# Second norm's tiles of the first sequence turned through DRAM instead of on TensorE, its pieces of the first two sequences stored a place later, and the late loads of MLP input and residual issued in turns

## The chip, the cores and the metric

The kernel runs on one core of one Trainium2 chip. A core has TensorE (PE in the profile; its weight loads are PEld), VectorE (DVE), ScalarE (ACT), GpSimd (POOL) and SyncE (SP), which here issues every DMA of the program from one queue, in the order in which the program wrote them. The metric is the device time of one execution in microseconds (us), the median of several runs. Lower is better.

## The reference, cut to what matters

The input x has 4 sequences of 512 tokens with 512 features. Two residual blocks follow each other:

```python
x = x + attn(layernorm(x))          # gated linear attention, 4 heads of 128, chunks of 128 tokens
x = x + mlp(layernorm(x))           # the "second norm" feeds this

# attn, per chunk and head
q, k, v = x@Wq+bq, x@Wk+bk, x@Wv+bv;  k = k / max(norm(k), 1e-12)
alpha = sigmoid(x@Walpha+balpha);  beta = softplus(x@Wbeta+bbeta)
cla   = cumsum(log(alpha + 1e-6)) over the chunk
attn  = (q @ k.T) * beta * exp(cla - cla.T), causal
y     = attn @ v + (q @ state.T) * exp(cla)
state = state * exp(cla_end) + v.T @ (k * beta * exp(cla_end - cla))

# mlp: three matrices held as 4-bit codes with a scale for every 32 inputs
inter = gelu_tanh(x @ Wg.T) * (x @ Wu.T)     # 512 -> 4096
out   = inter @ Wd.T                          # 4096 -> 512
```

Everything is float32.

## The kernel before, in words

**Tiling.** A tile is 128 tokens of 512 features in float32 (256 KB): 4 tiles for each sequence, 16 in all. A chunk of the attention is one tile. `acc` is a tile of the running residual.

**Places.** The order of the work is written out by hand. The attention products of a sequence b are 12: four of v (`product_v`), four of q (`product_q`), four of k (`product_k`). Each is a place p; place 12b+j holds product j of sequence b. After each product, `behind(p)` (L775) issues the rest of the work of that place. The chunk (b, n) runs some places behind its products: `chunk_of(p)` (L748) gives it the three places from 9+12b+3n on. In the first, TensorE transposes k if need be and ScalarE makes the decay factors from a tile of running sums (`chunk_decay`, L599; the sums of the next chunk are loaded there by `load_sums`, those of a sequence's first chunk in product j = 7). In the second, `chunk_scores` (L658) forms q·k and multiplies it by the decay. In the third, `chunk_sums` forms y; `sums` adds it to the residual and stores that as `accd`, and `rest` starts the second norm. Steps can also be put off: `first_of[p]` is done at the beginning of place p (L783), `last_of[p]` at its end (L825).

**The norms.** `norm` (L330) takes statistics of a tile on VectorE and puts a `settle` step on a list; that step normalises the tile into `hn`. Then the tile has to be turned, so that features lie on partitions. There are two ways. Without `way`, the tile goes on the list `turned`, and `turn` (L374) has TensorE transpose its four 128x128 blocks into PSUM (L380) and calls `use`. With `way`, two VectorE instructions (L349) write the normalised tile with its 32-column blocks crossed, `cross` (L307) stores it to a DRAM tile of 512-byte runs (L310), loads it back in four DMAs of 64 KB (L315) two places later, and three places after that `turn_blocks` (L320) has VectorE transpose 32x32 blocks (L326). The first norm of sequences 1 to 3 takes the way through DRAM, and so do some tiles of k. The second norm of all sequences takes TensorE.

**The second norm's `use`** (`second_norm`, L402) splits the turned tile in three pieces whose sum is exact enough for TensorE's rounded float32 format: ScalarE makes `hi` (L406), VectorE `lo` and `mi` (L407, L408). Each piece is at once stored to `h2d` in DRAM (L410). A tile is turned two places after its `rest`, in the second place of the next chunk (`turn("f")` in L766 or L797), and its three stores stand in SyncE's queue at that spot.

**The MLP** (`mlp`, L955) runs in 35 rounds of up to four of the 32 tiles of the hidden layer for one sequence each, sequence i mod 4 in round i. Two of its places lie among the last attention products. `load_x` (L839) loads the 12 pieces of a sequence (3 kinds by 4 feature blocks, `jk`) for the next round, `residual` (L952) the four `acc` tiles. `gate_up` forms a gate and an up product (L853: `pa` from kinds 0 and 1, `pb` from kind 2), `down` the contribution to the output in PSUM (L897), which `add` and `subtract` (L905, L909) bring into `acc`. Round 1 is the first that uses `down`; its four `acc` tiles are loaded in `last` (L966), after the rest of the pieces for round 2.

**SBUF slots.** Tiles of SBUF come from a list of 42 places for one-tile objects (`one_k`, class `Homes`, L94): first freed, first given. A load into a slot waits until the slot's last user is done, which may be a DMA that still stores from it. PSUM has eight banks (L92), used in turns; the eight partial sums of `down` in a round take all of them.

Of the kernel before, what the change touches and what calls it, by code (L numbers as in the profile page):

```python
# [21 lines left out]
P = 128  # L22
# [13 lines left out]
def f32(t):  # L36
    return t.bitcast(F32)
# [3 lines left out]
def tile_gated_linear_attention__then__nvfp4_geglu(  # L41
# [19 lines left out]
    nc = tc.nc  # L61
    B, T, D = x.shape
    H = D // P
    NCH = T // P
# [12 lines left out]
    h2d = [  # L77
        [dram.tile([KC, P, T], F32, tag=f"h2_{b}_{j}", name=f"h2_{b}_{j}") for j in range(3)]
        for b in range(B)
    ]  # L80
# [40 lines left out]
    one_k = Homes("b", 42, [P, T], two_k)  # L121
# [4 lines left out]
    def heads(t):  # L126
        return t.rearrange("p (h d) -> p h d", d=P)
# [153 lines left out]
    def load(src, name):  # L281
        t = one_k.get(name)
        nc.sync.dma_start(f32(t), src)
        return t
# [13 lines left out]
    first_of, last_of = {}, {}  # L298
# [5 lines left out]
    def crossed(t):  # L304
        return t.rearrange("p (w k i) -> p k w i", w=KC, i=32)
# [14 lines left out]
    def turn_blocks(t, *to):  # L320

        new = f32(t).rearrange("p (a k i) -> p k a i", a=KC, i=32)
        done = 0
        for part in to:
            n = part.shape[1]
            nc.vector.transpose(part.rearrange("p k (a j) -> p k a j", j=32), new[:, done : done + n])  # L326
            done += n
        one_k.put(t)

    def norm(src, key, use, parts=1, within=None, way=None):  # L330


        st = small.tile([P, 6], F32, tag="st", name=f"st_{key}")
        nc.vector.bn_stats(st, f32(src))
        if within:
            within()
        mv = small.tile([P, 2], F32, tag="mv", name=f"mv_{key}")
        nc.vector.bn_aggr(mv, st)
        rs = small.tile([P, 1], F32, tag="rs", name=f"rs_{key}")
        nc.vector.tensor_scalar(rs, mv[:, 1:2], 1e-5, None, ALU.add)  # L340
        nc.gpsimd.tensor_tensor(rs, rs, minus_half[:, :1], ALU.pow)

        def settle():

            hn = one_k.get(f"hn_{key}")
            w = D // parts
            if way:
                for c in range(2):
                    nc.vector.tensor_scalar(  # L349
                        crossed(f32(hn)).rearrange("p (c two) w i -> p c two w i", c=2)[:, c],  # L350
                        f32(src).rearrange("p (c w i two) -> p c two w i", c=2, w=KC, two=2)[:, c],
                        mv[:, 0:1], rs, ALU.subtract, ALU.mult,
                    )
                one_k.put(src)
                cross(hn, key, way, place[0] + 1, place[0] + 4)
                one_k.put(hn)
                return
            for cols in (slice(i * w, (i + 1) * w) for i in range(parts)):
                nc.vector.tensor_scalar(
                    f32(hn)[:, cols].rearrange("p (c two j) -> p c two j", two=2, j=P),  # L360
                    f32(src)[:, cols].rearrange("p (c j two) -> p c two j", two=2, j=P),
                    mv[:, 0:1], rs, ALU.subtract, ALU.mult,
                )
            one_k.put(src)
            turned.append((hn, key, use))

        settled.append(settle)
# [34 lines left out]
    def second_norm(b, n, src):  # L402
        def use(tp):
            g = [one_k.get(f"g{j}_{b}_{n}") for j in range(3)]
            hi, lo, mi = g
            nc.scalar.activation(hi, tp, AF.Copy, scale=HI)  # L406
            nc.vector.tensor_tensor(lo, tp, f32(hi), ALU.subtract)  # L407
            nc.vector.scalar_tensor_tensor(mi, f32(hi), ONE_E, tp, ALU.mult, ALU.subtract)  # L408
            for j in range(3):
                nc.sync.dma_start(  # L410
                    h2d[b][j][:, :, n * P : (n + 1) * P].rearrange("k p t -> p k t"), heads(f32(g[j]))
                )
            one_k.put(*g)

        norm(src, f"f{b}_{n}", use)


    zs, ss = {}, {}
# [321 lines left out]
    for b in range(1, B):  # L740
        for n in range(NCH):
            p = 3 * NCH * (b - 1) + 3 * n - 1 if b > 1 else 2 + 3 * max(n - 1, 0)
# [3 lines left out]
    place, met, summed = [0], set(), []  # L746
# [92 lines left out]
    def load_x(i, which):  # L839
        if i < len(rounds):  # L840
            for j, k in which:
                x3[i].append(load(h2d[i % B][j][k], f"x_{i}_{j}_{k}"))
# [109 lines left out]
    def residual(i, which=range(NCH)):  # L952
        return [load(accd[i % B * NCH + n], f"acc_{i}_{n}") for n in which]

    def mlp():  # L955
        for i, r in enumerate(rounds):
            ts = range(i % B * NCH, (i % B + 1) * NCH)
            ms = tiles[i]
            inter = []
            a4 = residual(i) if i > 1 else None  # L960
            ahead = [0] if i >= B - 1 else [i] if i > 0 else []
            for q, mt in enumerate(ms):
                if q in ahead:
                    load_x(i + 1, jk[: 8 if i == 1 else 6])

                def last():  # L966

                    if q == len(ms) - 1:
                        one_k.put(*x3[i])
                        rest = jk[len(x3[i + 1]) :] if i + 1 < len(rounds) else []  # L970
                        if i == 1:

                            nonlocal a4
                            load_x(i + 1, rest)
                            a4 = residual(i)
                        else:
                            load_x(i + 1, rest)


                some = ((2, 0), (3, 2))[q] if i == 1 else (1, 1)  # L980
                inter.append((yield from gate_up(mt, x3[i], some, r + MC, last, f"{i}_{mt}", mt == ms[-1] and len(ms) < 3)))
                if mt == r and mt < tiles[-1][0]:
                    two_k.put(*wgu[mt])
            final = i + B >= len(rounds)
            dst = [of[t * P : (t + 1) * P, :] if final else accd[t] for t in ts]
            if i == 0:
                over = ms, inter
                continue
            if i == B:
                ms, inter = over[0] + ms, over[1] + inter  # L990
            down(ms, inter, a4, dst, f"{i}", i == len(rounds) - 1)
            if r >= 0 and r % 2 == 1 and r < tiles[-1][0]:
                two_k.put(*wd[r // 2])
            yield


    with tc.manual_schedule():
# [45 lines left out]
        p = 0  # L1043
# [95 lines left out]
```

## Time and profile before

| | |
|---|---|
| median of 3 runs | 1303.22 us (1302.1 to 1303.25) |
| the profiled execution | 1301.6 us, its span 1299.9 us |
| PE busy | 1288.6 us, 99% of the span |
| PEld / DVE busy | 1030.6 us (79%) / 968.1 us (74%) |
| ACT / POOL busy | 452.2 us (35%) / 113.5 us (9%) |
| mean granted TensorE clock | 0.998 |
| DMA | 250.24 MB, mean 193 GB/s |

The span runs from the first to the last instruction of the profiled execution; 1.7 us of its time lie around it. The page of the profile lists the chain of work that ended last, followed back from the last instruction. In the views quoted below, a group of instructions is named by its line of the kernel, its engine and operation, and the tiles that it writes and reads (`tp_f<-ident,hn_f` are the transposes of the second norm, `g` its pieces, `h` their store in DRAM, `x<-h` the MLP's loads of them, `sums<-rows` the loads of running sums, `acc<-acc` the loads of the residual). Times count from the span's start. "Busy" of PE is of modelled, overlapping matmuls.

The last tile of the second norm is turned at 280.4 us, beside the first rounds of the MLP; from there to the end the rounds repeat.

### The profile page before, as it was taken

To read this page: it belongs to the slowest core of one execution; us is meant where nothing else is said; L and a number is where in the kernel's file an instruction comes from. 1 tells how busy PE (TensorE), PEld (TensorE's weight loads), DVE (VectorE), ACT (ScalarE), POOL (GpSimd) and SP (SyncE) were. 2 spreads that over 40 slices of the span, in tenths; PEclk is the share of its full clock that TensorE was granted. 3 is DMA by queue.
4 is the path that set the end of the run, shared out by engine and by line. 5 is a ranking of instruction groups with operands and counts; after the bars stand their busy time and mean duration, and the time that the engine had idled before them with its cause. 6 is when DMAs were issued, how large, how long until landed. Compare 5 with 4: busy or idle time off the path is not lost.

```text
span 1299.9 us, 17044 instructions
## 1 busy us (share of the span) xinstructions
PE 1288.6 (99%) x5736; PEld 1030.6 (79%) x5736; DVE 968.1 (74%) x1581; ACT 452.2 (35%) x878; POOL 113.5 (9%) x179
## 2 busy tenths in 40 slices
PE   9999999999999999999999999999999999999998
PEld 6667576778888888888888888888888888887886
DVE  4577865877777777777777777777777777777566
ACT  2333335743333333333333333333333333332332
POOL 1526462400000000000000000000000000000000
PEclk9999999999999999999999999999999999999999
DMA  6556667976565656555555565656555555555473
GB/s 208 163 163 191 196 191 226 310 263 213 179 195 178 194 178 194 178 195 178 194 178 194 178 194 179 195 178 194 179 194 179 192 181 190 182 179 199 167 253 126
DMA packets 195383, 250.24 MB, mean 193 GB/s; under 512 B 16672, under 2 KB 93792, under 8 KB 195296
## 3 DMA queue, kind: packets, MB, share of 16 engines
q1 hardware_dynamic: 195296, 249.16, 59.3%
q8 instruction: 45, 0.74, 0.2%
q14 instruction: 42, 0.34, 0.1%
HBM read 191.91 MB, written 57.18 MB: 192 GB/s over the span
## 4 chain that ended last, share of the span: by engine, by line
PE 95%; DVE 2%; DMA 1%; ACT 1%; issue 0%; SPq 0%; POOL 0%; DVEq 0%; ACTq 0%; POOLq 0%
PE pa L853 35%; PE p_d L897 26%; PE pb L853 18%; PE pq L450 4%; PE pk L474 3%; PE pva L425 2%; PE pvb L432 2%; PE yp L717 1%; PE sp L663 1%; PE yp L719 1%; PE dp L688 1%; PE tp_f L380 0%; DMA sums<-rows 0%; DMA acc<-acc 0%; DMA x<-h 0%
## 5 line engine op out<-in xcount | busy, mean ns | idle before, releaser
L853 PE MATMUL pa<-x,wgu 128*128 128x512 f32 x2048 | 508.5, 390 | 0.1
L853 PEld LDWEIGHTS pa<-x,wgu 128*128 128x128 f32 x2048 | 384.7, 188 | 80.0 <-DVE acc L909 0.4
L897 PE MATMUL p_d<-wd,i 128*128 128x512 f32 x1542 | 357.3, 389 | 2.3 <-DVE xr L726 0.6
L897 PEld LDWEIGHTS p_d<-wd,i 128*128 128x128 f32 x1542 | 288.2, 188 | 65.8 <-DVE i L877 2.1
L858 ACT ACTIVATE t<-pb 128x512 f32<-128x512 f32 x256 | 151.2, 591 | 357.9 <-PE pb L853 354.0
L853 PE MATMUL pb<-x,wgu 128*128 128x512 f32 x1024 | 273.7, 389 | 0.0
L859 DVE TENSOR_TENSOR t<-pa,t 128x512 f32<-128x512 f32 x256 | 176.4, 689 | 81.7 <-ACT t L858 76.4
L853 PEld LDWEIGHTS pb<-x,wgu 128*128 128x128 f32 x1024 | 192.3, 188 | 40.2
L905 DVE SCALAR_TENSOR_TENSOR acc<-p_d,acc 128x512 f32<-128x512 f32 (+1 forms) x137 | 93.3, 681 | 127.4 <-PE p_d L897 124.0
L873 ACT ACTIVATE i<-t 128x512 fp32r<-128x512 f32 x128 | 81.1, 634 | 194.2 <-DVE t L870 191.1
L865 ACT ACTIVATE t<-t 128x512 f32<-128x512 f32 x128 | 81.1, 634 | 136.0 <-DVE t L859 136.0
L877 DVE TENSOR_TENSOR i<-t,i 128x512 fp32r<-128x512 f32 x128 | 88.3, 690 | 26.0 <-ACT i L873 24.2
L909 DVE TENSOR_TENSOR acc<-acc,p_d 128x512 f32<-128x512 f32 x135 | 92.8, 688 | 14.4 <-PE p_d L897 0.5
L870 DVE SCALAR_TENSOR_TENSOR t<-t,t 128x512 f32<-128x512 f32 x128 | 88.6, 692 | 4.3
L928 POOL TENSOR_TENSOR acc<-acc,last 128x512 f32<-128x512 f32 x1 | 1.3, 1295 | 1015.1 <-ACT last L927 1015.1
L878 DVE SCALAR_TENSOR_TENSOR i<-i,t 128x512 fp32r<-128x512 f32 x128 | 88.9, 694 | 0.0
L450 PE MATMUL pq<-hT,wq 128*128 128x512 f32 x128 | 57.6, 595 | 0.0
L474 PE MATMUL pk<-wk,hT 128*128 128x512 f32 x128 | 57.4, 592 | 0.0
L450 PEld LDWEIGHTS pq<-hT,wq 128*128 128x128 f32 x128 | 23.6, 190 | 24.1 <-issue 23.9
L474 PEld LDWEIGHTS pk<-wk,hT 128*128 128x128 f32 x128 | 23.2, 190 | 23.9 <-issue 23.9
L183 DVE TENSOR_TENSOR wgu<-wgu,wgu 128x1024 fp32r<-128x1024 f32 x32 | 38.9, 1215 | 0.0
L180 DVE SCALAR_TENSOR_TENSOR wgu<-wgu,w_gu 128x1024 fp32r<-128x1024 f32 x32 | 38.9, 1215 | 0.0
(120 smaller groups left out, 901.6 us busy)
## 6 DMA issues: line engine op xcount, KB each, us to landing
x<-h SPq DMA_DIRECT2D x420, 256.0 KB
acc<-acc SPq DMA_DIRECT2D x256, 256.0 KB
h<-g SPq DMA_DIRECT2D x48, 256.0 KB
x<-in_x SPq DMA_DIRECT2D x16, 256.0 KB
pk_gu<-in_gate_p SPq DMA_DIRECT2D x32, 128.0 KB
sc_gu<-in_gate_s SPq DMA_DIRECT2D x64, 64.0 KB
pk_gu<-in_up_p SPq DMA_DIRECT2D x32, 128.0 KB
sc_gu<-in_up_s SPq DMA_DIRECT2D x64, 64.0 KB
```

The costliest lines, as they stand in the source:

```text
L450: nc.tensor.matmul(pq, f32(wq[k // 2])[:, k % 2, h * P : (h + 1) * P], f32(hT[b][k // 2])[:, k % 2, :], start=(k == 0), stop=(k == KC - 1),)
L474: nc.tensor.matmul(pk, f32(hT[b][k // 2])[:, k % 2, n * P : (n + 1) * P], f32(wk[k // 2])[:, k % 2, :], start=(k == 0), stop=(k == KC - 1),)
L853: nc.tensor.matmul(o, w3[j][:, k % 2, c * P : (c + 1) * P], x[j * KC + k], start=(j == js[0] and k == 0), stop=(j == js[-1] and k == KC - 1),)
L858: nc.scalar.activation(f32(t), pb, AF.Copy, scale=-1.0 / ONE_E)
L859: nc.vector.tensor_tensor(f32(t), pa, f32(t), ALU.add)
L865: nc.scalar.activation(f32(g), f32(g), AF.Gelu_apprx_tanh, scale=ONE_E)
L870: nc.vector.scalar_tensor_tensor(f32(u), f32(g), ONE_E, f32(u), ALU.mult, ALU.mult)
L877: nc.vector.tensor_tensor(il, f32(u), f32(ih), ALU.subtract)
L878: nc.vector.scalar_tensor_tensor(im, f32(ih), ONE_E, f32(u), ALU.mult, ALU.subtract)
L897: nc.tensor.matmul(banks[key_][:, part], inter[i][j][:, n * P : (n + 1) * P], wd[ms[i] // 2][j][:, ms[i] % 2, part], start=(i == 0 and j i ...
L905: nc.vector.scalar_tensor_tensor(a, banks[n, False, part.start][:, part], ONE_E, a, ALU.mult, ALU.add)
L909: nc.vector.tensor_tensor(a, a, banks[n, True, 0], ALU.subtract)
```

## The change

1. The second norm of sequence 0 gets a `way`: its four tiles are normalised by the two crossed instructions, stored to DRAM, loaded back in four DMAs each, and turned by VectorE into a new tile `h2T`, from which `use` makes the pieces. The second norm of the other three sequences is still turned on TensorE.
2. The three stores of the pieces are a step of their own. For sequences 0 and 1 it is put at the beginning of the next place, and the pieces' slots are freed there; for sequences 2 and 3 it is done at once, as before.
3. In round 1 of the MLP, the last four pieces of `x` for round 2 and the four `acc` tiles are loaded two and two in turns. Before, all four pieces were loaded ahead of the four `acc` tiles.

```diff
-            for j in range(3):
-                nc.sync.dma_start(
-                    h2d[b][j][:, :, n * P : (n + 1) * P].rearrange("k p t -> p k t"), heads(f32(g[j]))
-                )
-            one_k.put(*g)
-
-        norm(src, f"f{b}_{n}", use)
+
+            def store():
+                for j in range(3):
+                    nc.sync.dma_start(
+                        h2d[b][j][:, :, n * P : (n + 1) * P].rearrange("k p t -> p k t"), heads(f32(g[j]))
+                    )
+                one_k.put(*g)
+
+
+            if b < 2:
+                first_of.setdefault(place[0], []).append(store)
+            else:
+                store()
+
+        def way(t):
+            whole = one_k.get(f"h2T_{b}_{n}")
+            turn_blocks(t, heads(f32(whole)))
+            use(f32(whole))
+            one_k.put(whole)
+
+        norm(src, f"f{b}_{n}", use, way=way if b < 1 else None)
...
-                            load_x(i + 1, rest)
-                            a4 = residual(i)
+                            a4 = []
+                            for s in range(0, NCH, 2):
+                                load_x(i + 1, rest[s : s + 2])
+                                a4 += residual(i, range(s, s + 2))
```

## The prediction

> **What bounds the kernel.** The page first, its slices and its chain:
>
> ```profile
> PE   9999999999999999999999999999999999999998
> ...
> PE 95%; DVE 2%; DMA 1%; ACT 1%; issue 0%; SPq 0%; POOL 0%; DVEq 0%; ACTq 0%; POOLq 0%
> ```
>
> TensorE sets the time. So an edit is worth TensorE work taken from a stretch that the chain spends on PE, or a stall of PE that goes; all else costs nothing until it makes PE wait. Next the chain in order of time, where a piece's second number is its us:
>
> ```profile
> 60.09 1.73 PE pvb L432 x8
> 61.81 0.44 PE tp_f L380 x4
> 62.25 0.89 PE sp L663 x8
> ```
>
> Pieces join without a gap: four transposes are charged 0.44. Sequence 0's other three tiles stand so at 76.27, 91.55 and 105.41. From 7 us to 155 us no other engine is on the chain. Two later places leave PE. The first, at 155 to 169 us, in the chain and in SP's timeline:
>
> ```profile
> 155.89 2.75 SPq L410 DMA_DIRECT2D h<-g  x3
> 158.73 0.69 SPq L579 DMA_DIRECT2D sums<-rows  x1
> ```
>
> ```profile
> 158.73 5.16 DMA sums<-rows
> ...
> 168.14 0.69 DVE dm L674
> 168.83 0.04 issue
> 168.87 1.16 PE yp L717 x8
> ```
>
> The first sums of sequence 2 are issued only behind three stores of pieces, which took SP 2.75 us. They land at 163.89; decay, pieces and scores follow late, and y's eight matmuls take 1.16 where the same piece takes 0.89 at 111.07. With the short gap before them PE loses some 0.4 us. The second, at 255 to 268 us, in the timeline (in brackets the idle time before, and who ended it) and in the busy times by stretch (PE, PEld, DVE, ACT and POOL busy; the last three numbers are granted clock, DMA share and GB/s):
>
> ```profile
> 255.72 2.26 SPq L283 DMA_DIRECT2D x<-h  x4
> 258.03 1.85 SPq L283 DMA_DIRECT2D acc<-acc  x4
> 262.87 0.69 DVE L905 SCALAR_TENSOR_TENSOR acc<-p_d,acc 128x512 f32<-128x512 f32 x1 [3.43 <-DMA acc<-acc]
> 263.62 0.66 PE L593 MATMUL tpk<-ident,k 128*128 128x128 f32 x4 [2.57 <-DVE acc L905]
> 264.41 3.68 PE L853 MATMUL pa<-x,wgu 128*128 128x512 f32 x8
> 270.09 2.10 PE L853 MATMUL pa<-x,wgu 128*128 128x512 f32 x8
> ```
>
> ```profile
> 260.00:262.00 2.00, 1.04 (x5) 0.54 (x3) 0.00 (x0) 0.00 (x0) 0.07 (x1) 1.00 0.97 316
> 262.00:264.00 2.00, 0.39 (x4) 0.39 (x4) 1.03 (x2) 0.00 (x0) 0.00 (x0) 1.00 0.94 324
> 264.00:266.00 2.00, 1.86 (x7) 1.34 (x6) 1.90 (x4) 1.68 (x2) 0.00 (x0) 0.62 0.69 260
> 266.00:268.00 2.00, 2.00 (x7) 1.54 (x6) 1.79 (x4) 1.99 (x6) 0.45 (x1) 0.53 0.36 136
> ```
>
> Round 1's partial sums hold all eight PSUM banks; the next transposes wait 2.57 us for the first `add`, which waits for the first `acc` tile, issued behind four pieces of x while the DMA engines are full (share 0.94 to 0.97). Then the clock drops to half for 3.4 us (0.62 and 0.53 over two stretches of 2 us: 0.76 + 0.94 us lost), so eight matmuls take 3.68 instead of about 1.85.
>
> **Part 1, the turning.** Removed from PE: 16 transposes, four pieces of 0.44: **1.76 us**, all on the path. Two durations compete for a transpose: the group row of L380 has 273 ns mean, and the Trainium skill ("TensorE: Matmul & The Clock Gate", Part 4) gives some 275 ns in a kernel's context, which would make 16 x 0.275 = 4.4 us. But that is latency; transposes overlap, and the chain charges 0.44 / 4 = 0.11 us each. I take 1.76.
>
> Added for each tile: VectorE two L349 (470 ns) for one L359 (574), plus one transpose of 128x512 (L326 on kT: 701), pieces from SBUF instead of PSUM at no difference (L877/L878: 690 and 694, against 689 and 676): 0.37 + 0.70 + 0.02 = 1.09 us, 4.4 us for four. VectorE is busy 54.97 of the 72.90 us from 57.5 to 130.4, so it has 17.9 us to hide this in; uncovered it costs 4.4. ScalarE +0.04 a tile (L873 634 against L406 593). SP one store (L310, 0.38) and four loads (L315, 2.25 together): 2.6 us a tile, 10.5 in all, where its issues fill 50.9 of the same 72.9 us. DMA 0.5 MB a tile, 2 MB in 60 us on top of 163 to 196 GB/s: 33 GB/s more, below the 310 that a slice reaches. The order on VectorE helps: the pieces of sequence 0 no longer stand ahead of `dm` (L407 and L408, 1.37 us before L674) but behind it, at the place's end.
>
> The skill speaks against this part: "VectorE: DVE Perf Modes", "The three transpose paths", warns that a strided DMA copy for a transpose is 19 times slower than the DMA's own transposer. Here the copy only moves 512-byte runs and VectorE turns inside blocks; the trace's own store waits 61.47 to 65.64 for its four loads to begin, 4.2 us, with three more places until the turning. By the rule, at 19 times the section's 1.3 us, an estimate of 25 us for one block, the transposes at the head of VectorE's queue would come some 10 us late (three places are about 14 us) and hold PE up by as much, 40 us for four tiles; by the row they are in time and the sum is as above. I take the row.
>
> **Part 2, the stores.** At 155.89 the three stores leave the spot ahead of the sums, which so issue up to 2.8 us earlier and the stall at 168.8 goes: **0.4 us**. In their new spot the stores stand ahead of `accd`'s store and the way stores, which wait for later VectorE work anyhow; sums of the following chunk come behind them, with three places of slack. Pieces hold three slots a place longer. Readers of `h2d` come much later (x<-h from 199.5 us). Bounds: 0 to 0.5.
>
> **Part 3, the turns.** Moved: two x pieces go behind two `acc` tiles. The first `acc` takes over the spot of the third piece (issued at 257.19 in the trace) and its slot: 0.84 us earlier in issue than 258.03. In transfers two of 256 KB fewer lie ahead; at 316 to 324 GB/s each is 0.82 us, so 1.64 us. Lower bound 0.84 (issue alone), upper 1.64 + 0.2. I take **1.65**, since the full DMA engines set the landing. What is late next: the last two x pieces, now landing where `acc` 0 and 1 did, about 262.8 and 263.6; their first reader, `pb`, would start near 264.5, so some 0.9 us cover it, and a miss costs the miss.
>
> Does the clock's 1.7 us come back too? The skill ("TensorE: Matmul & The Clock Gate", Part 1) has the gate close after an idle window of some 3.4 us; here it closed after 2.57 us of wait, so the measurement decides that less is enough, while 0.9 us may leave it open. By the page's wording this wait was never the cause and the 1.7 stays. It hardly matters: if the clock stays up, PE meets the next `hn_f` (L359), which VectorE reaches only after its eight adds (268.44, done 269.17; the transposes begin 269.63). Adds 1.2 to 1.65 us earlier plus 0.46 of slack give 1.7 to 2.1. So both ways come out near 1.65, up to 2.1.
>
> **Sum.** 1.76 + 0.4 + 1.65 = 3.8 us. The profiled execution took 1301.6 (span 1299.9, 1.7 around it) and would take 1297.8. It stands 1.6 below the median, for which I subtract the same: 1303.2 - 3.8 = **1299.4 us**, its own range 1298.0 to 1300.6.
>
> **The rivals.** *Part 3 is hidden.* VectorE was late before (PE waits 0.44 and 0.59 us for it at 255.8 and 257.1), `acc` transfers share the engines with later ones, or the late x pieces hold up `pb`. Then 1.76 + 0.4 stay: 1301.1. For it: `acc` 0 and later loads run beside each other on 16 engines; against it: the 3.43 us wait names `acc` alone. Chance 0.2.
>
> *More than counted.* The earlier `dm`, the open clock and a calmer SP add up, with the upper bounds: 1.76 + 0.5 + 2.1, and one more half-clock window of 1.7, which could be what the median has over the profiled execution: 6.1, so 1297.1. Chance 0.1.
>
> *The change doesn't do what it says:* PE waits elsewhere for what it no longer transposes (banks, sums), and no stall is moved: 1303. Chance 0.1.
>
> *Slower: SP's queue.* In place 19 eight way loads instead of four stand ahead of sequence 1's first sums. They had landed by 102.69, when ACT's L608 began; POOL reached the mask L612 only at 106.04 (held by kw and vb, so 2.1 us of cover), and `dm`, moved ahead of the pieces, could end 3.4 us before y's matmuls at 110.8. From 5.4 us of delay on PE idles microsecond for microsecond, with a half-clock window (1.7) behind it. I count 2.25 us for four more loads minus 2.8 for the three stores that leave, so no delay; but the loads wait for landings, 4.2 us at most today, with two tiles at once perhaps 1 more. With the 3.8 gained, slower by 0.2% needs 3.8 + 2.6 - 1.7 = 4.7 us of idling, a delay of 10.1; 1306 to 1308. Chance 0.1.
>
> **How the numbers follow.** Some 0.2% (2.6 us) is what a measurement here can tell from no change. The likeliest case has 0.5, with 0.1 for more: faster 0.6. Hidden and nothing: same 0.3. Slower 0.1. The range leaves out half of the slower case and the tail of the fastest: 1297.0 to 1303.4.
>
> **What would show it.** Right: L380's tp_f x48 and no chain piece of it before 117 us; L326 on a new tile x4 at about 0.7; no `sums<-rows` in the chain at 158; the wait of L905 for `acc` under 2 us, and either a clock of 1.00 at 264 or a wait for hn_f. Wrong: PE waiting for `dm` or `sums` between 90 and 130 us, a `pb` that waits for x<-h near 264, or a half-clock window at a new place.

## The result, and the profile after

The changed kernel takes **1315.27 us** in the median (1313.94 to 1315.82), beside 1302.66 (1301.81 to 1303.25) for the kernel before in the same session: a ratio of **1.0098, 95% interval 1.0086 to 1.011**. It is slower by 12.6 us where the prediction had it faster by 3.8, and it lies 12 us above the predicted range. The profiled execution took 1313.94 us, with a span of 1312.2 (1301.6 and 1299.9 before).

Lines of the kernel behind the edit move down by 14: L425 is now L439, L674 is L688, L717 is L731, L905 is L919. L310, L315, L326, L359 and L380 stay; the store of pieces, L410, is L412.

The page of the kernel after, its slices, the clock's slices and the chain's shares by engine:

```profile
PE   9998899989999999999999999999999999999998
...
PEclk9999899999999999999999999999999999999999
...
PE 90%; DMA 5%; DVE 2%; SPq 1%; ACT 1%; issue 1%; POOL 0%; DVEq 0%; ACTq 0%; POOLq 0%
...
L439 PE MATMUL pva<-wva,hT 128*128 128x264 f32 x128 | 33.2, 405 | 10.4 <-DVE hT L326 10.0
```

Before, every slice but the last was a 9, and PE had 95% of the chain. Now the fourth and fifth slices are an 8 (98 to 164 us), and so is the ninth (262 to 295, part 3's place); the clock dips in the fifth (131 to 164), and DMA's share of the chain has gone from 1 to 5%. One group names the cause: PE waits 10.0 us for `hT`, once.

To sum it up, I took for each matmul the time from the end of the matmul before it to its own end, less the median of that for its form; what is left over is PE's lost time. It is 11.58 us before and 25.41 after, 13.83 more. Less the transposes that are gone (L380 has 64 of them instead of 80; 16 x 0.109 = 1.75), and with 0.27 more of tail, that is the 12.3 us between the spans. Of the added loss 11.9 us lie at one place, 135 to 140 us, and 0.8 near 115; the region of part 3 (250 to 285 us) loses 8.5 where it lost 7.4.

That place, in the chain in order of time (start, us, what):

```profile
126.03 0.57 SPq L412
...
126.64 4.64 DMA h<-g
...
131.47 0.72 DVE h2T L326
...
134.31 1.52 DVE g L408
135.84 0.36 DVE hT L326
...
136.24 3.89 PE pva L439 x8
```

and in the timeline (in brackets the idle time before, and who ended it):

```profile
122.90 0.69 DVE L688 TENSOR_TENSOR dm<-sp,dm 128x512 f32<-128x512 f32 x1
125.84 0.39 PE L733 MATMUL yp<-state,qc 128*128 128x128 f32 x2
131.47 0.71 DVE L326 STREAM_TRANSPOSE h2T<-way_f 128x512 f32<-128x512 f32 x1 [7.88 <-DMA h<-g]
135.76 0.76 DVE L326 STREAM_TRANSPOSE hT<-way_a 128x256 f32<-128x256 f32 x2
136.24 3.89 PE L439 MATMUL pva<-wva,hT 128*128 128x264 f32 x8 [10.01 <-DVE hT L326]
```

Read it from below. PE's next product needs `hT` of sequence 2, which VectorE turns at the end of a place. In VectorE's timeline the new turning of tile 3 of sequence 0 into `h2T` stands ahead of it. That waits 7.88 us, and not for its data: for a *store of pieces*. Following the list of free tiles through the program gives the reason: `h2T` of tile 3 is handed the slot of the `lo` piece of tile 2, which the program gave back when the store was queued. The store is issued only at 126.64 and lands at 131.28. Then the eight matmuls take 3.89 us instead of the 1.78 of before (126.77 to 128.55, with no wait ahead of them), as the clock is at half (us of the stretch; busy PE, PEld, DVE, ACT, POOL; granted clock, DMA share, GB/s):

```profile
134.00:136.00 2.00, 0.00 (x0) 0.00 (x0) 2.00 (x3) 1.80 (x5) 1.29 (x1) 0.50 0.11 33
136.00:138.00 2.00, 1.76 (x4) 1.45 (x5) 2.00 (x8) 0.00 (x0) 0.00 (x0) 0.50 0.39 104
138.00:140.00 2.00, 2.00 (x6) 1.49 (x6) 1.90 (x5) 0.00 (x0) 0.30 (x1) 0.50 0.68 233
```

Why was the store so late? SP's timeline after, and then before, at the same part of the program (the last column counts the issues of the row):

```profile
109.59 0.98 SPq L310 DMA_DIRECT2D way_f<-hn_f  x1
...
114.99 2.27 SPq L315 DMA_DIRECT2D way_f<-way_f  x4
117.37 2.70 SPq L315 DMA_DIRECT2D way_a<-way_a  x4
...
121.73 4.20 SPq L315 DMA_DIRECT2D way_k<-way_k  x4
126.03 2.30 SPq L412 DMA_DIRECT2D h<-g  x3
...
129.66 0.56 SPq L593 DMA_DIRECT2D sums<-rows  x1
```

```profile
110.78 2.28 SPq L315 DMA_DIRECT2D way_a<-way_a  x4
113.16 2.81 SPq L410 DMA_DIRECT2D h<-g  x3
...
121.95 0.51 SPq L579 DMA_DIRECT2D sums<-rows  x1
```

The same load of sums is issued 7.7 us later than before, at 129.66 instead of 121.95. The delay adds up from tile to tile: at the five loads of sums from 62 us on it is 0.8, 1.8, 3.3, 6.9 and 7.7 us. I use the last of these loads below as a mark of how late SP is. The waits of SP's queue from 57.5 to 130.4 us, the longest of before and of after (us in total, times, longest):

```profile
SPq L315 <- DMA way_a<-hn_a: 16.3, 5, 4.2
```

```profile
SPq L315 <- DMA way_f<-hn_f: 9.3, 4, 2.7
```

Before, SP stood 16.3 us at the head of its queue until the first norm's tiles had landed; these are part of the time that the prediction took for free. After, the loads of the new tiles wait there instead, 9.3 us, and those of the first norm, which come behind them, find their tiles landed.

From the loads of k at 57.4 us to the mark, SP's timeline adds up to 45.3 us of issues and 19.2 of standing before, 58.2 and 14.1 after. So the issues grew by 12.8 us (11.4 of them the 20 new DMAs), and the standing gave back only 5.1: that is the delay of 7.7.

### The profile page after: what moved, and what is told of

Its sections match the earlier page's. It is cut to its first block, busy times and chain, and to the rows that moved or that the text cites. A ratio compares the mean times of both kernels' runs of the same rounds, so it can differ in the third digit from the quotient of the medians.

```text
span 1312.2 us, 17054 instructions
## 1 busy us (share of the span) xinstructions
PE 1290.0 (98%) x5720; PEld 1031.2 (79%) x5720; DVE 974.9 (74%) x1589; ACT 452.4 (34%) x878; POOL 112.3 (9%) x179
## 4 chain that ended last, share of the span: by engine, by line
PE 90%; DMA 5%; DVE 2%; SPq 1%; ACT 1%; issue 1%; POOL 0%; DVEq 0%; ACTq 0%; POOLq 0%
PE pa L867 35%; PE p_d L911 25%; PE pb L867 17%; PE pq L464 3%; PE pk L488 3%; PE pva L439 2%; DMA x<-h 2%; PE pvb L446 2%; DMA h<-g 2%; SPq L315 1%; PE sp L677 1%; PE yp L731 1%; DMA x<-in_x 1%; PE yp L733 0%; PE dp L702 0%
## 5 line engine op out<-in xcount | busy, mean ns | idle before, releaser
L919 DVE SCALAR_TENSOR_TENSOR acc<-p_d,acc 128x512 f32<-128x512 f32 (+1 forms) x137 | 93.4, 683 | 127.7 <-PE p_d L911 123.5
L488 PE MATMUL pk<-wk,hT 128*128 128x512 f32 x128 | 57.4, 593 | 0.0
L439 PE MATMUL pva<-wva,hT 128*128 128x264 f32 x128 | 33.2, 405 | 10.4 <-DVE hT L326 10.0
```

The lines of the kernel that those rows point to most:

```text
L488: nc.tensor.matmul(pk, f32(hT[b][k // 2])[:, k % 2, n * P : (n + 1) * P], f32(wk[k // 2])[:, k % 2, :], start=(k == 0), stop=(k == KC - 1),)
L919: nc.vector.scalar_tensor_tensor(a, banks[n, False, part.start][:, part], ONE_E, a, ALU.mult, ALU.add)
```

## The experiments

Times are medians; the ratios are against the kernel before in the same session (1301.8 to 1303.1 us), and can differ a little from the quotient of the two medians.

### The three parts, one at a time

**Part 3 alone** (the kernel before with this edit only):

```diff
-                            load_x(i + 1, rest)
-                            a4 = residual(i)
+                            a4 = []
+                            for s in range(0, NCH, 2):
+                                load_x(i + 1, rest[s : s + 2])
+                                a4 += residual(i, range(s, s + 2))
```

> Part 3 alone on the kernel before (late x pieces and residual loaded two and two). The prediction's step says 1.65 us faster: ratio 0.9987, the wait of the first add for acc down from 3.4 to under 2 us. The rival from the changed kernel's trace: the first acc tile takes over the slot of the third x piece with that slot's wait for a store of pieces to land, so its load starts at most 0.8 us earlier and lands no earlier behind as many transfers: between 0.5 us faster and 1.5 us slower, the wait still 3 us or more.

Measured: 1300.94 us, ratio 0.9985 (0.9974 to 0.9996): 1.6 us faster by the medians, 2.0 by the ratio; span 1299.1. Its timeline and stretches, at the spot where the kernel before waited for `acc` and then ran at half clock:

```profile
261.94 0.69 DVE L905 SCALAR_TENSOR_TENSOR acc<-p_d,acc 128x512 f32<-128x512 f32 x1 [0.97 <-PE p_d L897]
262.69 0.66 PE L593 MATMUL tpk<-ident,k 128*128 128x128 f32 x4
268.98 0.66 PE L380 MATMUL tp_f<-ident,hn_f 128*128 128x128 f32 x4 [1.60 <-DVE hn_f L359]
```

```profile
264.00:266.00 2.00, 2.00 (x10) 1.63 (x10) 1.33 (x3) 1.99 (x4) 0.00 (x0) 1.00 1.03 394
266.00:268.00 2.00, 1.38 (x11) 1.11 (x9) 1.79 (x4) 1.56 (x4) 1.37 (x3) 1.00 0.64 246
```

The first `add` waits for PE and no longer for `acc`, the transposes behind it wait for nothing, the clock stays at 1.00, and PE meets `hn_f` 1.60 us early: what the prediction described.

**Part 2 alone** (the stores of sequences 0 and 1 as a step of the next place, the second norm on TensorE):

```diff
-        norm(src, f"f{b}_{n}", use, way=way if b < 1 else None)
+        norm(src, f"f{b}_{n}", use, way=None)
```

with part 3 undone as well.

> Part 2 alone: the second norm is turned on TensorE throughout, only the stores of the pieces of sequences 0 and 1 stand a place later. The prediction's step says 0.4 us faster (0.9997): no wait for the first sums of sequence 2. If the later stores themselves keep slots busy (stores in flight when the slot is written again), PE waits somewhere between 60 and 180 us and it is slower by 1 us or more.

Measured: 1301.72 us, ratio 0.9994 (0.9987 to 1.0001), span 1299.6; the 0.47 us lost at 165 us are gone from the profile. The size agrees with the 0.4 predicted; a ratio of 1 is not excluded.

**Part 1 alone** (stores at once, part 3 undone):

```diff
-            if b < 2:
+            if b < 0:
                 first_of.setdefault(place[0], []).append(store)
```

> Part 1 alone: sequence 0's second norm through DRAM, its stores at once. The prediction's step says 1.76 us faster. Slot theory (the stall of 10 us needs a late store and a slot taken back two places later): the stores are issued a place earlier, some 5 us, so the stall at sequence 2's first v product shrinks to 5 us or less and the time is 3 to 6 us above before. Queue theory (SyncE is full: the way loads wait for the way stores): stores that wait for their pieces in the queue make it later still, the stall stays at 8 us or more, 9 to 14 us above before.

Measured: 1316.6 us, ratio 1.0103 (1.0081 to 1.0125). The whole loss is here. The stall has other places: PE loses 8.4 us near 130 and 5.0 near 165. Its waits, and the longest wait of VectorE:

```profile
PE yp L731 <- DVE dm L688: 9.8, 3, 6.0
```

```profile
128.10 0.69 DVE L407 TENSOR_TENSOR g<-tp_f,g 128x512 fp32r<-128x512 f32 x1 [6.39 <-DMA h<-g]
```

Again a new tile, here a piece, whose slot a store still reads.

**Parts 1 and 2**, without part 3.

> Parts 1 and 2 without part 3. Both theories of the stall: it is all there, about 10 us of wait of PE for hT at the first v product of sequence 2 and 1.7 us of half clock; the time is that of the changed kernel less what part 3 costs, 1313 to 1316 us, 10 to 13 us above before.

Measured: 1317.85 us, ratio 1.0109 (1.0089 to 1.0129): the stall of the changed kernel, 10.0 us of PE for `hT` and 7.9 of `h2T` for a store. Against it the whole change (1.0098) is 1.4 us faster by the ratios, which is less than their noise (about 3 us): whether parts 2 and 3 gain inside the change isn't shown by the times.

**Parts 2 and 3**, the changed kernel with part 1 undone by the edit shown for part 2:

> Parts 2 and 3 of the change without part 1: no tile of the second norm goes through DRAM. The gains measured alone were 0.8 (part 2, stores a place later) and 1.6 us (part 3, turns), at places 90 us apart, so they should add: 2.4 us below the kernel before, near 1300.2, ratio 0.998. If part 3's gain needs the queue as it was in the kernel before, only one of them shows: 1301 to 1302 us. If part 2 is what hurts in the changed kernel: over 1305 us.

Measured: 1299.74 us, ratio **0.9977 (0.9964 to 0.999)**: 3.0 us faster than before, and the fastest version here with the right output. Its runs lie apart: six at 1299.0 to 1299.8 us, five at 1300.4 to 1303.8, the profiled one (1302.21) among the latter.

So part 1 costs some 13 us by itself (0.0103 x 1302.5 = 13.4). Two explanations stood at this point: A, tiles are handed out while a store still reads them; B, SP's queue is late, whatever tile is handed out.

### Which of the two: tiles, or SP's queue

**Tiles handed out later.** The changed kernel, but a tile that a DMA read last comes back to the list four places later:

```diff
+        def put_late(self, p, *ts):
+            for t in ts:
+                _, tag, whole = self.used.pop(id(t))
+                self.late.append((p, tag))
+
+        def age(self, p):
+            while self.late and (p - self.late[0][0] >= 4):
+                self.free.append(self.late.pop(0)[1])
...
-                one_k.put(*g)
+                one_k.put_late(place[0], *g) if b < 2 else one_k.put(*g)
```

(also for the sources and rows of tiles that go through DRAM; `get` takes a late tile when no other is free, and `age` is called at every place)

> The changed kernel in full, but a tile that a DMA was the last to read (pieces of sequences 0 and 1, sources and rows of the way tiles) comes back to the pool only four places later, or when nothing else is free. Same instructions on every queue, so SP stays as full and as late as in the changed kernel (its stores for tile 2 some 12 us behind PE). Theory A (what stalls is the reuse of a tile whose store is still on its way): the transpose into h2T of tile 3 no longer waits 7.9 us for a store, PE's wait for hT goes from 10.0 to under 2 us, the half-clock window behind it goes too: 1302 to 1305 us. Theory B (SP's queue is late, whatever tile is handed out): something else that SP brings late takes the stall's place, PE still loses 8 us or more between 110 and 140, 1311 to 1316 us.

Measured: 1316.28 us, ratio 1.0091 (1.007 to 1.0111). The wait for `hT` falls to 1.1 us, as A had it, but nothing is won. PE's and SP's waits in this kernel:

```profile
PE yp L743 <- DVE dm L700: 11.4, 3, 9.3
```

```profile
SPq L327 <- DMA way_f<-hn_f: 9.8, 4, 3.1
```

PE now waits 9.3 us for a `dm` that ends at 166 us. Behind it, the chain of this kernel goes through loads that SP issues:

```profile
151.17 5.33 DMA sc_gu<-in_gate_s
156.51 2.07 SPq L327
...
159.79 4.89 DMA xr<-in_x
...
165.53 0.61 DVE dm L700
```

The load of `xr` is issued at 159.79, where the kernel with part 2 alone issues it at 147.24, and the mark stands at 132.46. Tile reuse decides where the stall falls, not that there is one. A as the only cause is out.

**Loads a place later.** The changed kernel with

```diff
-                cross(hn, key, way, place[0] + 1, place[0] + 4)
+                cross(hn, key, way, place[0] + (2 if key[0] == "f" else 1), place[0] + 4)
```

> The changed kernel in full, but the four loads that bring a tile of the second norm back are issued one place (about 4.6 us) later, when its store has landed. Theory B in its form 'loads at the head of SP's queue wait for the way store to land': the 2.7 us waits of these loads go, SP catches up by about 2.7 us a tile, the stores of tile 2 are issued some 5 to 8 us earlier, and PE's wait for hT falls from 10.0 to under 4 us: 1303 to 1309 us. If SP is late only by the number of its issues (so many more DMAs a tile): SP stays as late, 1312 to 1316 us.

Measured: 1320.51 us, ratio 1.0126 (1.0102 to 1.0149): worse. SP's and VectorE's waits:

```profile
SPq L315 <- DMA way_a<-hn_a: 11.8, 4, 3.4
```

```profile
DVE h2T L326 <- DMA way_f<-way_f: 9.0, 2, 4.9
```

The edit didn't take a wait away: the next loads in the queue, the first norm's, wait for their own landing at the same spot (11.8 us where the changed kernel has 3.2 for them from 58 to 140 us). And the loads are now so late that VectorE waits for them. My expectation overlooked who stands next in the queue.

**Another queue.** The changed kernel with the new store and loads issued by ScalarE, the loads at the end of their place:

```diff
-        nc.sync.dma_start(way.rearrange("w p m -> p w m"), f32(src).rearrange("p (w m) -> p w m", m=P))
+        other = key[0] == "f"
+        queue_of = nc.scalar if other else nc.sync
+        queue_of.dma_start(way.rearrange("w p m -> p w m"), f32(src).rearrange("p (w m) -> p w m", m=P))
```

(the loads likewise)

> The changed kernel in full, but the way store and the four loads of the second norm's tiles are issued from ScalarE's queue, the loads at the end of their place. The DMA traffic is the same, SP's queue is as in the kernel before. Theory B (SP's queue): SP no longer falls behind, the stores of tile 2 are issued near 113 us as before, the stall for hT goes, 1300 to 1304 us, unless ScalarE, held by the loads' waits, is late for PE itself. Theory C (the 2 MB more of traffic slow every landing): PE still waits 8 us or more, 1311 to 1316 us.

Measured: 1318.69 us, ratio 1.0112 (1.0088 to 1.0135). PE's waits:

```profile
PE sp L679 <- ACT kT L612: 5.1, 2, 4.2
PE rps L576 <- ACT la L558: 4.7, 1, 4.7
```

The wait goes where the DMAs go: now it is ScalarE that comes late to its copy of k and to its logarithm. SP isn't on time either: it issues the fourth of the loads of sums at 116.33, where it was 104.75 before. So the run fits a queue held by loads, but it doesn't separate it from the traffic. The next runs do.

### Part 1 taken apart

**The DMAs alone.** The kernel before, with the transposes on TensorE, plus the store and four loads of each tile into a tile that nobody reads:

```diff
             turned.append((hn, key, use))
+            if key[:2] == "f0":
+                cross(hn, key, one_k.put, place[0] + 1, place[0] + 4)
```

> The kernel before, with the transposes of sequence 0 left on TensorE and their pieces as they were, plus only the DMAs of part 1: for each of the four tiles the store of its rows and, a place later, the four loads into a tile of the pool, which is given back three places later unread. VectorE and TensorE do nothing new; the output is unchanged. Theory B (SP's queue, filled by these 20 DMAs and the waits ahead of them): PE loses 10 us or more between 90 and 170, 1312 to 1320 us. Theory E (VectorE's 4.4 us of added work, and the later order of its pieces, are what is late): no more than 1 us, 1302.5 to 1304 us.

Measured: 1320.04 us, ratio 1.0136 (1.0116 to 1.0155). Twenty DMAs on whose data nothing waits cost 17.7 us (0.0136 x 1302.5). PE's waits and SP's:

```profile
PE yp L719 <- DVE dm L676: 9.6, 3, 5.4
```

```profile
SPq L315 <- DMA way_f<-hn_f: 9.7, 4, 2.8
```

**No DMAs.** Part 1 alone, with the tile kept in SBUF and turned there; it leaves out the exchange of blocks, so the values are in the wrong order:

```diff
-                cross(hn, key, way, place[0] + 1, place[0] + 4)
-                one_k.put(hn)
+                if key[0] == "f":
+                    last_of.setdefault(place[0] + 4, []).append(lambda: way(hn))
+                else:
+                    cross(hn, key, way, place[0] + 1, place[0] + 4)
+                    one_k.put(hn)
```

> Part 1 alone, without its DMAs: the normalised tile stays in SBUF and VectorE turns it inside its 32x32 blocks at the same place, but its blocks are not exchanged, so the second norm's values of sequence 0 are in the wrong order. TensorE does not transpose, VectorE and ScalarE do all that part 1 gives them; SP's queue is as in the kernel before. Theory B: only the 1.76 us that the prediction counted on TensorE remain, with the SP stall at 165 us as before: 1301 to 1302.5 us. Theory E: VectorE's added work alone makes PE wait 8 us or more, 1310 to 1316 us.

Measured: 1306.33 us, ratio 1.003 (1.0015 to 1.0045): 3.9 us slower, between the two expectations. Most of the loss goes with the DMAs, but the 1.76 us don't show either. VectorE's waits show tile reuse again (the tile held in SBUF takes a slot longer):

```profile
DVE g L410 <- DMA h<-g: 5.6, 2, 3.2
```

**Loads that don't wait.** Part 1 alone with all its DMAs, but the loads read the input (so the second norm's values are wrong):

```diff
+                block = way[:, a * 32 : (a + 1) * 32, :]
+                if key[0] == "f":
+                    block = tile_of(0)[:, a * P : (a + 1) * P].rearrange("(w r) m -> w r m", w=KC)
-                nc.sync.dma_start(f32(t)[:, a * P : (a + 1) * P], way[:, a * 32 : (a + 1) * 32, :])
+                nc.sync.dma_start(f32(t)[:, a * P : (a + 1) * P], block)
```

> Part 1 alone, with all of its DMAs in their places, but the four loads of a tile read 64 KB each of the input x instead of the tile just stored, so they need not wait for its landing; the second norm's values of sequence 0 are wrong. As many issues on SP and as much traffic as in part 1 alone. Theory B1 (the wait for the store's landing at the head of SP's queue, 9.0 us in four places, is what makes SP late): it goes, 1301 to 1306 us. Theory B2 (the number of issues, some 10 us of SP's time, is enough): 1310 to 1317 us.

Measured: 1307.95 us, ratio 1.0048 (1.003 to 1.0066). With the same number of DMAs and the same bytes, 8.7 us of part 1's loss are gone by the medians, 7.2 by the ratios, and SP is on time: the timeline of SP here has the mark at

```profile
121.23 0.56 SPq L596 DMA_DIRECT2D sums<-rows  x1
```

where it stands at 121.95 before, at 130.80 in part 1 alone, and at 132.16 with the DMAs alone. This is the strongest reading: with as many DMAs, SP is late only where their loads wait for a store's landing at the head of its queue. Loads that don't wait are issued while the first norm's tiles land, for which SP stands only 4.5 us between the loads of k and the mark, where it stood 13.3 before. From those loads to the mark SP needs 9.2 us less than in part 1 alone: 3.7 less of standing and 5.5 less of issuing, for the same 88 issues. Why these take less time when no load waits isn't shown. 1307.95 lies just above the 1301 to 1306 expected for B1, so something else remains.

### Are the two together the whole cause?

The changed kernel with the later tiles (as above), **and no DMAs** for part 1:

> The changed kernel in full, but without part 1's DMAs (blocks of sequence 0's second norm turned, but not exchanged, so its values are in the wrong order), and with tiles that a DMA read last handed out four places later. VectorE does all of part 1's work. Two-cause theory: the 3.8 us that remained without the DMAs were tile reuse, so nothing waits for a store of pieces any more; parts 2 and 3 give 2.8 us as measured together, part 1 its 1.76: 1298 to 1299.5 us. Theory E (VectorE's added 4.4 us are late by themselves): 1302 to 1306 us.

Measured: 1303.14 us, ratio 1.0002 (0.9989 to 1.0016). The profiled execution took 1298.85, with only 1.4 us lost near 150 us, as the two-cause theory expected, but it is the shortest of twelve; the others reach from 1299.2 to 1305.9. **The same kernel, profiled again:**

> The changed kernel without part 1's DMAs and with tiles handed out later, profiled again. If its executions differ by what happens between 57 and 175 us (part 1's places), the profile of an execution above 1302 us shows PE losing 2 us or more there, waiting for dm or hT; if by part 3's place, the loss is between 250 and 285 us.

Measured: 1299.32 us, again one of the short executions; it loses 1 us near 150. What the longer ones lose is in no trace, but the mean clock of each run is on record: 0.995 to 0.999 in the eight above 1302 us, 1.0 in three of the four below and 0.998 in the other. The means differ by 0.0022, an estimate of 2.9 us out of the 4.6 between the two groups. So the longer ones ran in part at half clock; behind which waits stays open, and with it whether the two causes are the whole.

The later tiles **and loads that don't wait**:

> The changed kernel in full, but the four loads of a tile read the input x (they wait for no landing; the second norm's values of sequence 0 are wrong), and tiles that a DMA read last are handed out four places later. All of part 1's issues and traffic and all its VectorE work stay. Two-cause theory: both causes are gone, PE loses no more than 1 us between 90 and 170: 1298 to 1301 us. If the number of issues (10 us of SP) or the traffic counts by itself: 1304 us or more.

Measured: 1306.21 us, ratio 1.002 (1.0004 to 1.0035), above the 1298 to 1301 of the two-cause theory. One stall remains, 5.3 us of PE for a `dm` near 155 us, whose chain goes back through SP:

```profile
134.74 5.91 SPq L427 DMA_DIRECT2D h<-g  x6
...
146.05 0.46 SPq L608 DMA_DIRECT2D sums<-rows  x1
```

In the kernel with later tiles and no DMAs the same six stores stand at 130.60 (5.42 us) and the same load of sums at 142.15, both some 4 us earlier. So the number of DMAs isn't free.

Later tiles **and loads a place later**, the edits shown above together:

> The changed kernel in full with its right result: the four loads of a tile come a place later, when its store has landed, and tiles that a DMA read last are handed out four places later. Two-cause theory: if the loads' wait at the head of SP's queue is gone and no tile is reused early, near e15, 1299 to 1303 us. But a place later alone left 11.8 us of waits for the first norm's tiles in SP's queue, as the kernel before has; if these, with the issues of part 1 on top, are what makes SP late, it stays at 1310 to 1320 us.

Measured: 1320.83 us, ratio 1.0143 (1.0128 to 1.0158): as with the loads a place later alone, and for the same reason (10.6 us of SP for the first norm's landings, 12.1 of `h2T` for its loads).

**VectorE's work alone.** Parts 2 and 3, with TensorE's transposes, plus two VectorE transposes for each tile of sequence 0, at the end of a place, into a tile that nobody reads:

```diff
+            def extra():
+                t = one_k.get(f"extra_{n}")
+                for w in (KC, KC // 2):
+                    nc.vector.transpose(
+                        f32(t)[:, : w * P].rearrange("p (k a j) -> p k a j", k=w, j=32),
+                        f32(mi)[:, : w * P].rearrange("p (a k i) -> p k a i", a=KC, i=32),
+                    )
+                one_k.put(t)
+
+            if b < 1:
+                last_of.setdefault(place[0], []).append(extra)
```

> Parts 2 and 3 of the change, TensorE's transposes of sequence 0 and all DMAs as in the kernel before; added alone, for each of the four tiles and at the end of the place that makes its pieces, are two VectorE transposes into a tile that nobody reads (128x512 and 128x256, some 1.06 us together, 4.2 us in all; part 1 adds 1.09 a tile). If VectorE's added work costs time by itself (theory E): 2 us or more above parts 2 and 3 alone, 1302 to 1305 us. If VectorE hides it, as the prediction had it: 1299.5 to 1301 us.

Measured: 1302.3 us, ratio 1.0004 (0.9995 to 1.0012), where parts 2 and 3 alone have 0.9977. So 4.5 us of VectorE work (four transposes of 684 ns and four of 445) cost about 0.0027 x 1302 = 3.5 us. In the timeline of PE, two places show it:

```profile
82.69 0.49 PE L742 MATMUL yp<-vb,dm 128*128 128x128 f32 x2 [0.68 <-DVE dm L699]
...
98.00 0.49 PE L742 MATMUL yp<-vb,dm 128*128 128x128 f32 x2 [0.66 <-DVE dm L699]
```

These are as long as one transpose, and in the kernel with parts 2 and 3 alone PE doesn't wait there. The profile accounts for 1.9 us of lost time at the two; the rest of the 3.5 is in no trace. This work is a stand-in: it has the size of part 1's, but not its places.

### The bill of part 1

Differences of ratios, times 1302.5 us:

| term | from | us |
|---|---|---|
| TensorE's transposes gone | profile | -1.8 |
| VectorE's added work | VectorE's work alone, less parts 2 and 3 (1.0004 - 0.9977) | +3.5 |
| tiles reused under a store, and what else remains without DMAs | no DMAs (0.0030), less the two rows above | +2.2 |
| issues and traffic of 20 DMAs | loads that don't wait, less no DMAs (1.0048 - 1.0030) | +2.3 |
| loads waiting for landings at SP's head | part 1 alone, less loads that don't wait (1.0103 - 1.0048) | +7.2 |
| sum: part 1 alone | 1.0103 | +13.4 |

Each of the differences is uncertain by 2 to 4 us (the intervals of two ratios, in squares): 7.2 is clear of zero, 3.5 is too, 2.2 and 2.3 by themselves are not. That the rows add up to 13.4 proves nothing, since the 2.2 is what the other rows leave. The 2.3 has a second pair of the same size, the two kernels with later tiles (1.0020 - 1.0002), not clear of zero by itself either. And the terms don't add freely: the DMAs alone cost 17.7, more than the 9.5 of their two rows. What makes the difference is open. So is the order on VectorE (turning `hT` ahead of `h2T`), which wasn't tried.

## Why the prediction was wrong, step by step

**Part 1, TensorE: right.** 16 transposes went, and with them 1.75 us. The chain's 0.11 us for each, and not the 273 ns of the group's row or the 275 ns of the Trainium skill ("TensorE: Matmul & The Clock Gate", Part 4), was the right duration: 16 x 0.109 is what the matmul ends show.

**Part 1, SP: this step failed.** "10.5 in all, where its issues fill 50.9 of the same 72.9 us" costed SP's part at nothing, as if 22 us were free. Of these, 16.3 were waits at the head of the queue for the first norm's tiles to land, so that 72.9 - 50.9 - 16.3 = 5.7 us were left for 10.5. The wait was in the prediction's hands (4.2 us, quoted as proof that a tile comes back in time) and was used for the data's delay alone. Loads that wait for no landing could have used part of that time, as the run with such loads shows; the new loads waited 9.3 us themselves. Of the 12.8 us by which SP's issues grew, only 5.1 came out of its standing; it was 7.7 us late at the mark, and the loads' waits are worth 7.2 us of the kernel's time.

**Part 1, VectorE: failed too, by less.** "17.9 us to hide this in" was an average over the stretch. The work stands at the end of a place, ahead of the next `dm`, and in the stand-in 3.5 us of 4.5 came through. "The order on VectorE helps" was half the picture: the turning at the place's end stands ahead of `hT`, which PE needs first thing in the next.

**Part 1, slots: not asked.** The prediction noted that "Pieces hold three slots a place longer", but not from where the new `h2T` would get its tile. At that place 15 tiles are free instead of 19, and the oldest free one was still being stored from. Before, pieces took slots of stored pieces too, and VectorE had no such wait; with SP late, such a reuse turned into the 7.88 us of VectorE and the 10.0 of PE.

**The warning of the skill** ("VectorE: DVE Perf Modes", "The three transpose paths"), 19 times slower for a strided copy (where the innermost stride of the destination is large, as the page has it): the trace's row was rightly preferred. In the changed kernel no turning waits for its loads; `h2T` takes 0.70 us, as counted. The loss came by a way on which the rule is silent.

**Part 2: borne out in the trace** where it stood alone (the stall at 168.8 gone, 0.4 predicted and 0.47 lost there before); its time, 0.8 by the ratio, is not clear of zero. **Part 3: right**, alone: 1.65 predicted, 1.6 by the medians (0.5 to 3.4 by the interval), both signs there. Together they give 3.0 us, against 2.05 predicted. In the changed kernel, though, part 3's wait is not gone. Chain, timeline and stretches of the kernel after:

```profile
265.31 5.36 DMA h<-g
...
270.73 3.94 DMA acc<-acc
```

```profile
275.50 0.66 PE L607 MATMUL tpk<-ident,k 128*128 128x128 f32 x4 [2.92 <-DVE acc L919]
```

```profile
276.00:278.00 2.00, 1.86 (x7) 1.36 (x6) 1.53 (x3) 1.79 (x2) 0.00 (x0) 0.65 1.00 380
278.00:280.00 2.00, 2.00 (x6) 1.58 (x5) 1.89 (x3) 1.88 (x6) 0.56 (x1) 0.50 0.84 321
```

The first `acc` takes the slot that the third piece of x had, as predicted, and that slot waits for a store of pieces, 5.36 us; the half-clock window comes back with it.

**The rivals.** "Slower: SP's queue" had the mechanism, loads that wait for landings, at a chance of 0.1. Its size was off: it allowed "perhaps 1 more" us for two tiles at once, looked at place 19 alone, where the delay would be made up, and ended at 1306 to 1308. Over four tiles the delay adds up instead, to 7.7 us, and it is VectorE's order and the tile list that bring it to PE, some 15 us further on than that place. Of the listed signs of being wrong, the half-clock window at a new place appeared; PE waited for `hT`, which wasn't on the list.

## What to carry to other kernels

In a queue that works in order, time in which its head waits for a landing is free only for DMAs that need not wait themselves: count issues plus landing waits before you add a store and its own load to it, and look at who stands behind. When an edit takes a new buffer from a "first freed, first given" list, ask whose buffer it gets and whether a DMA still reads from it; a late queue turns that into a wait on a compute engine. A share of busy time says little about cover: what counts is what stands directly ahead of the instruction that the bound engine waits for next.

## What the runs showed of the hardware

- **The length of a wait alone didn't decide whether the clock falls.** PE's waits of 2.57 us (before) and 2.92 us (after) were each followed by 3.41 us at half clock (0.62 and 0.53, 0.65 and 0.50 over two stretches of 2 us), and so was one of 2.05 us with the loads a place later. A wait of 2.56 us in parts 1 and 2 without part 3 (109.23 to 111.79 us) was not: the clock stayed at 1.00 from 110 to 116. After 1.60 us (part 3 alone) and 0.68 us (VectorE's work alone) it stayed at 1.00 too. The Trainium skill names an idle window of some 3.4 us ("TensorE: Matmul & The Clock Gate", Part 1); here shorter waits were enough.
- **The half-clock stretches lie on a grid.** In the clock records of every trace here with more than one, they start whole multiples of 3.413 us apart; in the changed kernel at 129.83 us (10.24 us long, three times 3.413) and 276.61 (43 times 3.413 later). On this grid the wait of 2.57 us lies almost wholly within one period (261.07 to 264.48), and the one of 2.56 us across two (the border is at 110.67). So a wait's place on the grid seems to count, but it isn't the whole: parts 2 and 3 alone have a half-clock stretch from 260.08 us, and the two waits before it that the trace shows are of 0.46 and 0.59 us.
- **The time of an issue varies.** The same four loads of k took SP 2.89 us at 117.56 before and 4.20 us at 121.73 after, the store of a tile between 0.37 and 0.98 us. Why isn't shown; that the queue is fuller after is only a guess.
- **Moving dependent loads to another queue moved the delay:** with ScalarE issuing the new store and loads, ScalarE stood idle for 9.07 us up to 89.80, its issues of three such loads taking 4.07 of them, and was late for PE by 4.2 and 4.7 us.
